# Side matmuls of a four-layer vision stack given all 128 columns and rows of the TensorE array

## The chip, the cores and the metric

The kernel runs on one core of a Trainium2 chip. Five engines work side by side: TensorE multiplies matrices (PE in the profile, its weight loads PEld), VectorE (DVE), ScalarE (ACT) and GpSimd (POOL) work element by element, and SyncE (SP) issues the transfers (DMA). Each engine takes its instructions in the order of the program and stops at one whose inputs are not there. The metric is the device time of the whole kernel in microseconds. Three runs before the change took 17867.69, 17889.07 and 17892.29 us; the median, 17889.07, is the time before.

## What is computed

Eight images of 48 x 48 positions and 96 channels go through four layers, each with a group norm before it and a residual around it. Layers 0 and 3 are two-dimensional state space models, layer 2 is a set of one-dimensional ones along rows and columns, and layer 1 is a small two-layer network on an image that is made wider and lower again by fixed filters. Cut to what matters:

```python
# layers 0 and 3
xz = einsum('bhwc,ec->bhwe', x, in_proj_w); xc, z = split(xz, 2)
xc = silu(depthwise_conv3x3(xc) + conv_b)                       # 192 channels
xs = four directions over the positions
dts, Bs, Cs = split(einsum('bkdl,kcd->bkcl', xs, x_proj), [6, 22])
delta = softplus(einsum('bkrl,kdr->bkdl', dts, dt_projs) + bias)
h = h * exp(delta * A) + (delta * u) * B                        # 16 states a channel
y = sum over the states of h * C, + u * D
y = layer_norm(sum of the four directions) * silu(z)
out = einsum('bhwd,cd->bhwc', y, out_proj_w)
# layer 2: for each of four directions
xi, z = split(x @ in_w); xi = silu(conv1d(xi)); the same scan; y * silu(z) @ outp_w; then @ out_w
# layer 1
h = up(x) @ W1.T; h = c0 + c1 * h + c2 * h * h; out = down(h @ W2.T)
x = x + layer(group_norm(x))                                    # each of the four in turn
```

All numbers are float32.

## The kernel before

The 192 inner channels are held as two halves of 96 (`DH`). The positions of an image are cut into five blocks of 480 or 384 (`BLKS`). With eight images and four directions each scanned layer has 160 blocks.

`scans` (from L192) is the loop that all three scanned layers share. A block is worked in four turns, a turn being six units of 128 partitions by one block (32 channels by 4 states). In a turn ScalarE makes the decay `ps_da` by an exponential (L296), VectorE makes part of the input products `dbu` (L272) and runs the scan in place over two units at a time (L304), GpSimd makes the rest of the input products (also L272) and multiplies the scanned states by C (L310), and TensorE sums over the states in `reduce` (from L318): three matmuls with the 0/1 matrix `w_red`, each on 32 columns of the array (L330), and a fourth with weights of zero on the remaining 32 (L332). The sum `ps_y` of a half block is opened by one matmul (L326), whose operands the layer gives in its `opening`: the skip term in the first direction (`dskip` or `diag`), and in layers 0 and 3 the sum so far through the identity in the other directions. When a half is done, the layer's `done` takes the result away: ScalarE copies it to `ysum` (L716), or in layer 2 VectorE multiplies it by the gate (L876).

Everything else on TensorE is work on the side of that loop, placed by hand at fixed slots of a block (`aside`, `stage1`, `side`): the convolutions (L536, L813, 128 rows by 128 columns already, since their weight rows are padded with zeros and a tap's columns run on into the next tap), the gates (L544, L854), the projection of u to B, C and the step size (`xp`, 96 rows by 38 columns, L675 and L830), the step size's own projection (`dtw`, 6 rows by 96 columns, L665 and L841), the output projections (L885, L607, L610), and the layer norm's mean and spread (L565, L577, L597). In layers 0 and 2 a `Guest` puts layer 1's matmuls into banks that are free in a slot: among them `narrow` (L1117), 128 rows by 73 columns over 96 elements.

TensorE takes all of this in program order. So a sum over states behind a side matmul waits for it, and a side matmul behind a sum waits for GpSimd's product. A float32 matmul stands in the trace as two loads of weights and two matmul records.

The weights lie in tiles of their own (`w_l_in`, `w_l_xp`, `dtw`, `dskip`, `diag`, `wnb`, `wo`) with 96 partitions, or 6. The activations that they meet, `u` and `ysum` (`big`, three buffers), `ub` (three), `bcl` (one), have as many partitions as they have rows.

Of the kernel before, what the change touches and what calls it, by code (L numbers as in the profile page):

```python
# [16 lines left out]
L = H * W  # L17
# [84 lines left out]
def vss_stack_kernel(ctx: ExitStack, tc: tile.TileContext, i: dict, out: bass.AP):  # L102
# [20 lines left out]
    wc = weights(const, ("gmat", "ident", "red"))  # L123
# [4 lines left out]
    mean = const.tile([DH, DH], F32, tag="mean", name="mean")  # L128
    nc.gpsimd.memset(mean, 1.0 / (2 * DH))
# [62 lines left out]
    def scans(dirs, order, restart, on_pool, a, pools, ps, stage1, opening, done, side, tail, ahead=None, guest=None):  # L192
# [125 lines left out]
        def reduce(t, sub):  # L318

            b, q = turns[t]  # L320
            n = b.n
            half, slot = q // 2, 2 * (q % 2) + sub
            if slot == 0:
                ys[b, half] = ps("y", 1)
                lhsT, rhs = opening(b, half)
                nc.tensor.matmul(ys[b, half][:DH, :n], lhsT=lhsT, rhs=rhs, start=True, stop=False)  # L326
            y = ys[b, half]
            hc = units(dbus[t], b, 3 * sub, 3 * sub + 3)
            for g in range(3):
                nc.tensor.matmul(y[32 * g:32 * g + 32, :n], lhsT=wc["red"][:, :32], rhs=hc[:, g, b.at], start=False, stop=(slot == 3))  # L330

            nc.tensor.matmul(y[DH:, :n], lhsT=wc["red"][:, 32:], rhs=hc[:, 2, b.at], start=(slot == 0), stop=(slot == 3))  # L332
            if slot == 3:
                ends.append((b, half))
            if sub == 1:
                dbus.pop(t)
# [101 lines left out]
    def scan_pools(stack):  # L438
        def pool(name, bufs, **kw):
            return stack.enter_context(tc.tile_pool(name=name, bufs=bufs, **kw))  # L440
        ps = pool("ps", 1, space=PSUM)

        def psum(tag, bufs, n=512):
            return ps.tile([P, n], F32, tag=tag, name=f"ps_{tag}", bufs=bufs)

        pools = {"dd": pool("dd", 3), "bc": pool("bc", 1), "dbu": pool("dbu", 4),
                 "dds": pool("dds", 1), "bcl": pool("bcl", 1),
                 "dr": pool("dr", 4, space=DRAM)}
        return pools, psum
# [31 lines left out]
    def ss2d(l, xin, xout, guest=None):  # L481
# [5 lines left out]
        wt, big, zp, lnp, xio = pool("wt", 1), pool("big", 3), pool("z", 1), pool("ln", 2), pool("xio", 1)  # L487
# [8 lines left out]
        w = weights(wt, [f"{l}_{n}" for n in ("in", "cb", "xp", "dtb", "a", "d", "nw", "nb", "out")])  # L496
        dtw = wt.tile([NBC, NK, 2, DH], F32, tag="dtw", name="dtw")
        nc.sync.dma_start(dtw[2 * NS:], i[f"{l}_dtw"])
# [4 lines left out]
        dskip = wt.tile([DH, 2, DH], F32, tag="dskip", name="dskip")  # L503
        for half in range(2):
            nc.scalar.activation(dskip[:, half, :], wc["ident"], AF.Identity, scale=dsum[:, half:half + 1])
# [3 lines left out]
        nc.vector.tensor_mul(taps, taps, w[f"{l}_in"][:, :2 * DH].unsqueeze(1).to_broadcast([DH, 9, 2 * DH]))  # L509

        wnb = wt.tile([DH, 2, C], F32, tag="wnb", name="wnb")
        for half in range(2):
            nc.scalar.activation(wnb[:, half, :], w[f"{l}_out"][:, half, :], AF.Identity, scale=w[f"{l}_nb"][:, half:half + 1])
        us, yss, zs = {}, {}, {}
# [8 lines left out]
        def conv(b, blks, behind=lambda step: step()):  # L523
            if blks[0] == BLKS[0]:
                us[b] = big.tile([DH, 2, L], F32, tag="big", name="u")
                zs[b] = zdr.tile([DH, 2, L], F32, tag="z", name="zd")
            for r0, nr in blks:
                n = nr * SEG
                for half in range(2):
                    for slot in range(7):  # L530
                        if slot == 2:
                            pu = side_psum()
                        for tap in ((), (), (0, 1), (2, 3), (4, 5), (6, 7, 8), ())[slot]:
                            dy, dx = tap // 3, tap % 3
                            at = (2 * tap + half) * DH
                            nc.tensor.matmul(pu[:, :n], lhsT=flat[:, at:at + P],  # L536
                                             rhs=xpad[:, r0 + dy:r0 + dy + nr, dx:dx + W],
                                             start=(tap == 0), stop=(tap == 8))
                        if slot == 6:
                            got = {}  # L540

                            def gate():
                                got["z"] = ps("s1", 1)
                                nc.tensor.matmul(got["z"][:DH, :n], lhsT=w[f"{l}_in"][:, (2 + half) * DH:(3 + half) * DH],  # L544
                                                 rhs=xpad[:C, 1 + r0:1 + r0 + nr, 1:1 + W], start=True, stop=True)
                            behind(gate)
                        yield slot < 2
# [7 lines left out]
        def post(b, blks=BLKS):  # L555
# [4 lines left out]
            for r0, nr in blks:  # L560
# [3 lines left out]
                for half in range(2):  # L564
                    nc.tensor.matmul(pm[:DH, :n], lhsT=mean, rhs=y[:, half, s], start=(half == 0), stop=(half == 1))  # L565
# [20 lines left out]
            for r0, nr in blks:  # L586
# [8 lines left out]
                for c in range(n // CH):  # L595
                    at = r0 * W // CH + c
                    nc.tensor.matmul(pr[:DH, c * CH:(c + 1) * CH], lhsT=var[:, at:at + 1].to_broadcast([CH, DH]),  # L597
                                     rhs=wc["ident"], start=True, stop=True)
# [7 lines left out]
                for half in range(2):  # L606
                    nc.tensor.matmul(po[:C, :n], lhsT=wnb[:, half, :], rhs=z[:, half, :n], start=(half == 0), stop=False)  # L607
                yield
                for half in range(2):
                    nc.tensor.matmul(po[:C, :n], lhsT=w[f"{l}_out"][:, half, :], rhs=y[:, half, s],  # L610
                                     start=False, stop=(half == 1))
# [46 lines left out]
        def stage1(b):  # L658
            n = b.n
            u = b.view(us[b.job], dirs[b.k][0])  # L660
            got = {}

            def raw(half):
                got["p"] = ps("s1", 1)
                nc.tensor.matmul(got["p"][:DH, :n], lhsT=dtw[2 * NS:, b.k, half, :], rhs=b.bcl[2 * NS:, :n],  # L665
# [6 lines left out]
            def s0():  # L672
                got["p"] = ps("s1", 1)
                for half in range(2):
                    nc.tensor.matmul(got["p"][:NBC, :n], lhsT=w[f"{l}_xp"][:, b.k, half, :], rhs=u[:, half],  # L675
                                     start=(half == 0), stop=(half == 1))

            def s1():
                b.bcl = pools["bcl"].tile([NBC, BMAX], F32, tag="bcl", name="bcl")
                nc.scalar.copy(b.bcl[:, :n], got["p"][:NBC, :n])  # L680
# [23 lines left out]
        def so_far(b, half):  # L704
            if b.job not in yss:
                yss[b.job] = big.tile([DH, 2, L], F32, tag="big", name="ysum")
            return b.view(yss[b.job][:, half], dirs[b.k][0])

        def opening(b, half):

            if b.k == 0:
                return dskip[:, half, :], b.view(us[b.job][:, half], False)
            return wc["ident"], so_far(b, half)

        def done(b, half, y):
            nc.scalar.copy(so_far(b, half), rows(y[:DH], b.n))  # L716
# [18 lines left out]
    def lines(xin, xout, guest):  # L735
# [5 lines left out]
        wt, xpool, up, gp = pool("wt", 1), pool("x", 2), pool("u", 3), pool("gated", 1)  # L741
# [26 lines left out]
        w = weights(wt, [f"l2_{n}" for n in ("inz", "cb", "xp", "dtb", "a", "d", "outb")])  # L768
        dtw = wt.tile([NBC, NK, 2, DH], F32, tag="dtw", name="dtw")
        nc.sync.dma_start(dtw[2 * NS:], i["l2_dtw"])  # L770
        a = w["l2_a"]
        negexp(a)
        flat = broadcast(wt, "l2_cw")
        taps = flat[:DH, :NK * 4 * 2 * DH].rearrange("p (k t e) -> p k t e", k=NK, t=4)
        diag = wt.tile([DH, NK, 2, DH], F32, tag="diag", name="diag")
        wo = wt.tile([DH, NK, 2, C], F32, tag="wo", name="wo")
# [20 lines left out]
        def stage1(b):  # L797
# [9 lines left out]
            def conv(half):  # L807
                def run():
                    got["u", half] = ps("sa" if half else "sb", 1)
                    for tap in range(4):  # L810
                        off = tap - 3 if not rev else 3 - tap
                        at = ((b.k * 4 + tap) * 2 + half) * DH
                        nc.tensor.matmul(got["u", half][:, :n], lhsT=flat[:, at:at + P],  # L813
# [3 lines left out]
            def s2():  # L817
                b.ub = up.tile([DH, 2, BMAX], F32, tag="ub", name="ub")
# [8 lines left out]
            def s3():  # L827
                got["p"] = ps("sa", 1)
                for half in range(2):
                    nc.tensor.matmul(got["p"][:NBC, :n], lhsT=w["l2_xp"][:, b.k, half, :], rhs=b.ub[:, half, :n],  # L830
                                     start=(half == 0), stop=(half == 1))

            def s4():
                b.bcl = pools["bcl"].tile([NBC, BMAX], F32, tag="bcl", name="bcl")
                nc.scalar.copy(b.bcl[:, :n], got["p"][:NBC, :n])

            def s5():
                s4()
                for half in range(2):
                    got[half] = ps("sb" if half else "sa", 1)  # L840
                    nc.tensor.matmul(got[half][:DH, :n], lhsT=dtw[2 * NS:, b.k, half, :], rhs=b.bcl[2 * NS:, :n],  # L841
# [9 lines left out]
            def s7():  # L851
                for half in range(2):
                    got["z", half] = ps("sb" if half else "sa", 1)
                    nc.tensor.matmul(got["z", half][:DH, :n], lhsT=w["l2_inz"][:, b.k, half * DH:(half + 1) * DH],  # L854
                                     rhs=shifted(0)[:C], start=True, stop=True)
# [4 lines left out]
            def s8():  # L860
                b.zb = up.tile([DH, 2, BMAX], F32, tag="zb", name="zb", bufs=2)
# [5 lines left out]
        def opening(b, half):  # L867
            return diag[:, b.k, half, :], b.ub[:, half, :b.n]
# [3 lines left out]
        def done(b, half, y):  # L872
# [8 lines left out]
            def project():  # L881
                got["o"] = ps("sa", 1)
                t = gated.pop(b)
                for h in range(2):
                    nc.tensor.matmul(got["o"][:C, :n], lhsT=wo[:, b.k, h, :], rhs=t[:, h, :n], start=(h == 0), stop=(h == 1))  # L885
# [34 lines left out]
    class Guest:  # L920
# [54 lines left out]
        def items(self):  # L975
# [54 lines left out]
            for b in range(nb):  # L1030
# [80 lines left out]
                def narrow(n, j0, j1):  # L1111
                    j1 = min(j1, bands[n][1])

                    def run(p):
                        for j in range(j0, j1):
                            for m in range(NM):
                                nc.tensor.matmul(p[:UG, (j - j0) * C:(j - j0 + 1) * C], lhsT=hq[:, m, j * UG:(j + 1) * UG],  # L1117
# [164 lines left out]
```

## Time and profile before

| what | before |
|---|---|
| median of three runs | 17889.07 us |
| profiled execution, time and span | 17892.97 us, 17891.2 us |
| VectorE: scan L304, products L272 | 11823.5 us x5760, 3828.8 us x2880 |
| GpSimd: L310 | 10071.8 us x3840 |
| ScalarE: exponential L296 | 7424.3 us x11520 |
| TensorE: sums over states L330, L332 | 4741.8 us x23040, 4705.9 us x7680 |
| TensorE: openings L326 | 764.5 us for the sums so far, x960 |
| TensorE: L665, L675 | 952.0 us x1280, 837.5 us x1280 |
| transfers | 2843.63 MB, mean 159 GB/s |

The counts of TensorE's lines are records, two a matmul. The records overlap: four sums over states on different columns run at once, so the busy times of single lines add up to more than the engine's 14657 us. The stretches of time that are named below are counted from the start of the span: layer 0 lasts until about 6075 us, layer 2 until about 12325 us, layer 3 to the end; layer 1 is worked beside layers 0 and 2. A row of a table of stretches ends in four numbers: the granted clock of TensorE as a share of full speed, the share of the transfer engines that is busy, and GB/s; a number with (x...) is busy time with its count of instructions. A wait reads: who waited <- for whom: us in total, times, longest.

### The profile page before, as it was taken

The page shows a single profiled execution, that of the slowest core. Times are in us where ns is not written, and L with a number is a line of the kernel's source. Part 1 is how long each engine was busy: PE and PEld are TensorE (multiplying, and loading weights), DVE is VectorE, ACT ScalarE, POOL GpSimd, SP SyncE. Part 2 cuts the span into 40 slices and gives each one's busy share as a digit, 9 for nine tenths or more (in the row PEclk, how much of TensorE's full clock was granted, in tenths as well). Part 3 has the DMA queues.
Part 4 walks back from the last instruction along what each step waited for, and adds up shares of the span by engine and source line. Part 5 has one row for each costly group of instructions (what it writes and reads, how often), then busy time and mean ns, then how long its engine had stood idle before and what let it go on. Part 6 is the DMA issues. An engine that isn't in the chain of part 4 may idle for free. (4 is left out here: it accounts for less than half of the span.)

```text
span 17891.2 us, 168509 instructions
## 1 busy us (share of the span) xinstructions
PE 14657.1 (82%) x53740; PEld 4413.6 (25%) x53740; DVE 15977.6 (89%) x9976; ACT 13880.5 (78%) x20932; POOL 15155.4 (85%) x7999
## 2 busy tenths in 40 slices
PE   6878888878787788888888888987778778778776
PEld 1223232323232322222222222222122222222221
DVE  7998999898888788787888889996999999999998
ACT  6877878878787677787777778786878778778776
POOL 7988888888888677787777778886999999999998
PEclk7778777878786788888888888888677777777776
DMA  4555545454545334443443444443455455455454
GB/s 141 176 166 171 172 165 170 162 178 159 168 159 174 131 137 153 137 150 133 152 144 140 144 146 156 154 154 124 170 173 173 169 174 176 168 176 177 169 175 142
DMA packets 887917, 2843.63 MB, mean 159 GB/s; under 512 B 353468, under 2 KB 421788, under 8 KB 760206
## 3 DMA queue, kind: packets, MB, share of 16 engines
q1 hardware_dynamic: 887022, 2832.85, 46.7%
q8 instruction: 421, 6.90, 0.2%
q14 instruction: 474, 3.88, 0.1%
HBM read 2384.40 MB, written 448.17 MB: 158 GB/s over the span
## 5 line engine op out<-in xcount | busy, mean ns | idle before, releaser
L304 DVE TENSOR_TENSOR_SCAN dbu<-ps_da,dbu 128x968 f32<-128x968 f32 (+3 forms) x5760 | 11823.5, 2074 | 923.6 <-ACT ps_da L296 757.6
L310 POOL TENSOR_TENSOR dbu<-dbu,bc 128x1440 f32<-128x1440 f32 (+1 forms) x3840 | 10071.8, 2635 | 2349.7 <-DVE dbu L304 2264.9
L296 ACT ACTIVATE ps_da<-dd,w_l_a 128x484 f32<-128x484 f32 (+3 forms) x11520 | 7424.3, 649 | 2511.4 <-DVE dbu L304 2282.1
L330 PE MATMUL ps_y<-dbu,w_red 128*32 128x480 f32 (+1 forms) x23040 | 4741.8, 731 | 1238.5 <-POOL dbu L310 1225.2
L332 PE MATMUL ps_y<-dbu,w_red 128*32 128x480 f32 (+1 forms) x7680 | 4705.9, 731 | 0.0
L272 DVE TENSOR_TENSOR dbu<-dd,ps_b 128x962 f32<-128x962 f32 (+5 forms) x2880 | 3828.8, 1329 | 270.3 <-ACT ps_b L253 160.7
L272 POOL TENSOR_TENSOR dbu<-dd,bc 128x481 f32<-128x481 f32 (+5 forms) x2240 | 3914.8, 1763 | 23.3 <-DMA dd<-dd 18.9
L330 PEld LDWEIGHTS ps_y<-dbu,w_red 128*32 128x32 f32 x23040 | 797.7, 126 | 5072.2 <-POOL dbu L310 2976.6
L253 ACT COPY ps_b<-bc 128x482 f32<-128x482 f32 (+3 forms) x2720 | 1448.3, 532 | 209.9 <-DVE dbu L272 164.4
L536 PE MATMUL ps_side<-xpad,w_l_cw 128*128 128x480 f32 (+1 forms) x2880 | 1466.0, 651 | 42.1 <-ACT g_room L1109 12.7
L296 ACT ACT_TABLE_LOAD x993 | 1274.0, 1283 | 17.4
L665 PE MATMUL ps_s<-bcl,dtw 6*96 6x480 f32 (+1 forms) x1280 | 952.0, 835 | 290.6 <-ACT dds L669 133.5
L813 PE MATMUL ps_sb<-xpad,w_l_cw 128*128 128x480 f32 (+1 forms) x1280 | 879.0, 839 | 90.4 <-ACT g_room L1109 33.7
L326 PE MATMUL ps_y<-ysum,w_ident 96*96 96x480 f32 (+1 forms) x960 | 764.5, 887 | 207.5 <-ACT ysum L716 203.3
L470 POOL TENSOR_TENSOR dds<-dds,u 96x960 f32<-96x960 f32 (+1 forms) x320 | 706.8, 2209 | 209.7 <-ACT dds L693 209.3
L675 PE MATMUL ps_s<-u,w_l_xp 96*38 96x480 f32 (+1 forms) x1280 | 837.5, 785 | 53.1 <-ACT g_room L1109 13.6
L813 PE MATMUL ps_sa<-xpad,w_l_cw 128*128 128x480 f32 (+1 forms) x1280 | 864.6, 826 | 0.1
L536 PEld LDWEIGHTS ps_side<-xpad,w_l_cw 128*128 128x128 f32 x2880 | 579.0, 216 | 890.5 <-issue 784.3
L332 PEld LDWEIGHTS ps_y<-dbu,w_red 128*32 128x32 f32 x7680 | 730.8, 126 | 0.0
L716 ACT COPY ysum<-ps_y 96x480 f32<-96x480 f32 (+1 forms) x640 | 472.0, 738 | 62.9 <-PE ps_y L332 61.5
L830 PE MATMUL ps_sa<-ub,w_l_xp 96*38 96x480 f32 (+1 forms) x640 | 344.3, 669 | 205.1 <-ACT ub L820 205.1
L669 ACT ACTIVATE dds<-ps_s,w_l_dtb 96x480 f32<-96x480 f32 (+1 forms) x640 | 405.5, 634 | 132.8 <-DMA dd<-dds 84.1
(236 smaller groups left out, 12311.2 us busy)
## 6 DMA issues: line engine op xcount, KB each, us to landing
dd<-dd SPq DMA_DIRECT2D x512, 1452.0 KB
bc<-bcd SPq DMA_DIRECT2D x1536, 480.0 KB
dd<-dd SPq DMA_DIRECT2D x256, 1440.0 KB
dd<-dds SPq DMA_DIRECT2D x512, 363.0 KB
dd<-dd SPq DMA_DIRECT2D x128, 1164.0 KB
bc<-bcd SPq DMA_DIRECT2D x384, 384.0 KB
dd<-dds SPq DMA_DIRECT2D x256, 360.0 KB
dd<-dd SPq DMA_DIRECT2D x64, 1152.0 KB
```

The source lines that it names most:

```text
L253: nc.scalar.copy(bps[t][:, :bcs[t][0].shape[1]], bcs[t][0])
L272: engine.tensor_mul(o, du, by.unsqueeze(1).to_broadcast([P, hi - lo, by.shape[1]]))
L296: nc.scalar.activation(da[:, at:at + b.m], b.got[half][:, u % 3, 0, :], AF.Exp, scale=a[:, b.k, ci:ci + 1])
L304: nc.vector.tensor_tensor_scan(db, da, db, 0.0, ALU.mult, ALU.add)
L310: nc.gpsimd.tensor_mul(h, h, bcs.pop(2 * t + sub)[1].unsqueeze(1).to_broadcast([P, 3, n]))
L326: nc.tensor.matmul(ys[b, half][:DH, :n], lhsT=lhsT, rhs=rhs, start=True, stop=False)
L330: nc.tensor.matmul(y[32 * g:32 * g + 32, :n], lhsT=wc["red"][:, :32], rhs=hc[:, g, b.at], start=False, stop=(slot == 3))
L332: nc.tensor.matmul(y[DH:, :n], lhsT=wc["red"][:, 32:], rhs=hc[:, 2, b.at], start=(slot == 0), stop=(slot == 3))
L536: nc.tensor.matmul(pu[:, :n], lhsT=flat[:, at:at + P], rhs=xpad[:, r0 + dy:r0 + dy + nr, dx:dx + W], start=(tap == 0), stop=(tap == 8))
L665: nc.tensor.matmul(got["p"][:DH, :n], lhsT=dtw[2 * NS:, b.k, half, :], rhs=b.bcl[2 * NS:, :n], start=True, stop=True)
L675: nc.tensor.matmul(got["p"][:NBC, :n], lhsT=w[f"{l}_xp"][:, b.k, half, :], rhs=u[:, half], start=(half == 0), stop=(half == 1))
L813: nc.tensor.matmul(got["u", half][:, :n], lhsT=flat[:, at:at + P], rhs=shifted(off), start=(tap == 0), stop=(tap == 3))
```

## The change

Each side matmul is given 128 weight columns, and 128 rows where the buffer of its moving operand has them. The weights of a layer move into one tile of 128 partitions, `square`, which is cleared and then filled; `wide(name, n)` hands out 128 columns from it, so that those past the matrix are the next matrix's or zeros, and their outputs are never read. The moving operands get 128 partitions, of which the upper 32 (for `bcl` all but 38) are zeros that are set once.

```diff
+    eye = const.tile([P, P], F32, tag="eye", name="eye")
+    nc.gpsimd.memset(eye, 0.0)
+    nc.sync.dma_start(eye[:C, :C], i["ident"])
...
+    def square(pool, sizes):
+        t = pool.tile([P, sum(sizes.values()) + P - DH], F32, tag="square", name="square")
+        nc.gpsimd.memset(t, 0.0)
+        at = dict(zip(sizes, np.cumsum([0, *sizes.values()]).tolist()))
+        def wide(name, n, rows_=P):
+            return t[:rows_, at[name] + n:at[name] + n + P]
+        def part(name, rows_=slice(0, DH)):
+            return t[rows_, at[name]:at[name] + sizes[name]]
+        return wide, part
+    def full(pool, tag, n, bufs):
+        made = []
+        for b in range(bufs):
+            t = pool.tile([P, n], F32, tag=f"{tag}{b}", name=f"{tag}{b}")
+            nc.gpsimd.memset(t[DH:], 0.0)
+            made.append(t)
+        return made
...
-                nc.tensor.matmul(ys[b, half][:DH, :n], lhsT=lhsT, rhs=rhs, start=True, stop=False)
+                nc.tensor.matmul(ys[b, half][:, :n], lhsT=lhsT, rhs=rhs, start=True, stop=False)
...
-            nc.tensor.matmul(y[DH:, :n], lhsT=wc["red"][:, 32:], rhs=hc[:, 2, b.at], start=(slot == 0), stop=(slot == 3))
+            nc.tensor.matmul(y[DH:, :n], lhsT=wc["red"][:, 32:], rhs=hc[:, 2, b.at], start=False, stop=(slot == 3))
...
+        pools["bcl"] = pool("bcl", 1).tile([P, BMAX], F32, tag="bcl", name="bcl")
+        nc.gpsimd.memset(pools["bcl"], 0.0)
...
+        wide, part = square(wt, {"in": 4 * DH, "xp": 2 * NK * NBC, "dtw": 2 * NK * DH, "out": 2 * C, "wnb": 2 * C, "dskip": 2 * DH})
+        bigs = full(pool("big", 1), "big", 2 * L, 3)
...
-                                nc.tensor.matmul(got["z"][:DH, :n], lhsT=w[f"{l}_in"][:, (2 + half) * DH:(3 + half) * DH],
-                                                 rhs=xpad[:C, 1 + r0:1 + r0 + nr, 1:1 + W], start=True, stop=True)
+                                nc.tensor.matmul(got["z"][:, :n], lhsT=wide("in", (2 + half) * DH),
+                                                 rhs=xpad[:, 1 + r0:1 + r0 + nr, 1:1 + W], start=True, stop=True)
...
-                nc.tensor.matmul(got["p"][:DH, :n], lhsT=dtw[2 * NS:, b.k, half, :], rhs=b.bcl[2 * NS:, :n],
+                nc.tensor.matmul(got["p"][:, :n], lhsT=wide("dtw", (2 * b.k + half) * DH), rhs=b.bcl[:, :n],
                                  start=True, stop=True)
...
-                    nc.tensor.matmul(got["p"][:NBC, :n], lhsT=w[f"{l}_xp"][:, b.k, half, :], rhs=u[:, half],
+                    nc.tensor.matmul(got["p"][:, :n], lhsT=wide("xp", (2 * b.k + half) * NBC), rhs=uall[:, half],
                                      start=(half == 0), stop=(half == 1))
...
-            return wc["ident"], so_far(b, half)
+            return eye, so_far(b, half)
...
+                            cols = min(P, UR * UG - j * UG)
                             for m in range(NM):
-                                nc.tensor.matmul(p[:UG, (j - j0) * C:(j - j0 + 1) * C], lhsT=hq[:, m, j * UG:(j + 1) * UG],
+                                nc.tensor.matmul(p[:cols, (j - j0) * C:(j - j0 + 1) * C], lhsT=hq[:, m, j * UG:j * UG + cols],
                                                  rhs=w2q[:, m, :], start=(m == 0), stop=(m == NM - 1))
```

Layer 2 is treated in the same way: `wide` stands for `w_l_inz`, `w_l_xp`, `dtw`, `diag` and `wo` (L854, L830, L841, L326, L885), with a tile `square` of 6480 columns, and its three `ub` buffers get 128 partitions. The output projection of the gate's constant part (L607) and that of layer 2 (L885) get 128 columns over 96 rows, since their moving operands keep 96 partitions; so does L597. The mean (L565) gets a 128 x 128 matrix, of which rows 0 to 95 hold 1/192. Not touched are the convolutions, the sums over states, the norm's small matmuls (L159, L577) and the guest's other matmuls.

## The prediction

> **What bounds the kernel now.** I read the page's busy shares and its clock row first, then the windows of the three stages, the waits of VectorE, the TensorE timeline of single stretches, and the granted clock window by window.
>
> ```profile
> span 17891.2 us, 168509 instructions
> PE 14657.1 (82%) x53740; PEld 4413.6 (25%) x53740; DVE 15977.6 (89%) x9976; ACT 13880.5 (78%) x20932; POOL 15155.4 (85%) x7999
> ...
> PEclk7778777878786788888888888888677777777776
> ```
>
> VectorE is the busiest and TensorE is granted only 0.777 of its clock on average. The stages (microseconds of the stretch, then busy time of PE, PEld, DVE, ACT, POOL, then the granted clock):
>
> ```profile
> 0.00:6075.00 6075.00, 4940.60 (x20066) 1675.09 (x20066) 5335.77 (x3311) 4705.11 (x7317) 5143.79 (x2898) 0.77 0.50 164
> 6075.00:12325.00 6250.00, 5396.06 (x18251) 1600.57 (x18250) 5413.92 (x3468) 4849.79 (x7082) 4907.29 (x2234) 0.83 0.41 146
> 12325.00:17891.00 5566.00, 4320.44 (x15424) 1137.93 (x15424) 5227.94 (x3199) 4325.55 (x6534) 5104.28 (x2869) 0.72 0.49 168
> ```
>
> VectorE idles 739 us in layer 0 (with layer 1 as guest), 836 us in layer 2 (guest too), 338 us in layer 3. TensorE's speed can win back only a part of these 1913 us. In layer 2 the waits of VectorE name it:
>
> ```profile
> DVE dbu L304 <- ACT ps_da L296: 327.4, 335, 2.8
> DVE gated L876 <- PE ps_y L332: 238.0, 127, 5.8
> DVE x L893 <- PE ps_sa L885: 181.3, 76, 4.5
> ...
> DVE x L891 <- PE ps_sa L885: 33.5, 31, 3.1
> ```
>
> The reader sees three places where VectorE stands for a matmul, and one for ScalarE. Following each wait for ScalarE back to the last gap in ScalarE's own queue, 185 us of layer 2's and 166 us of layer 0's end at a gap in which ScalarE itself waited for a matmul. Direct and through ScalarE, VectorE's idle time owed to TensorE is then 281 us in layer 0 (115 + 166), 638 in layer 2 (453 + 185), 88 in layer 3 (82 + 6): 1007 us.
>
> **Why TensorE is late.** The granted clock takes two values, 0.50 and 1.00, and changes on a grid of 3.41 us. A 128x128 convolution record of 480 elements follows the one before it after 403 ns at 1.00 and after 800 ns at 0.50. Of the 1007 us, 844 fall into windows at 0.50 or into the first two windows after a rise (259, 510 and 75 us by stage); 195 of the 215 us of L893 and L891 fall into the very first. So VectorE pays for what TensorE fell behind in slow windows.
>
> **What sets the clock.** Here a rule of the Trainium skill stands against a row. "TensorE: Matmul & The Clock Gate", section "The HAM clock gate", says that a monitor releases the clock after about one window of 3.4 us in which the PE was busy. By that rule zero rows and unread columns change nothing: a matmul streams as long with 96 columns as with 128, busy time stays, the clock stays 0.777, and the change costs only longer weight loads. The trace differs. Three windows of layer 3:
>
> ```profile
> 13292.94:13296.35 3.41, 3.41 (x5) 1.35 (x6) 3.41 (x3) 1.82 (x3) 3.41 (x3) 0.50 0.74 261
> 13296.35:13299.76 3.41, 3.41 (x6) 0.93 (x5) 3.41 (x3) 2.11 (x4) 3.02 (x3) 0.50 0.65 258
> 13299.76:13303.18 3.42, 3.42 (x14) 0.72 (x17) 3.42 (x4) 2.21 (x4) 3.42 (x2) 0.50 0.60 194
> ```
>
> What ran in them:
>
> ```profile
> 13292.85 3.52 PE L607 MATMUL ps_side<-zin,wnb 96*96 96x480 f32 x4
> 13296.16 3.41 PE L610 MATMUL ps_side<-ysum,w_l_out 96*96 96x480 f32 x4
> ```
>
> TensorE is busy throughout and the clock stays at 0.50. At the start of layer 3, one window full of 128*128 convolution is enough:
>
> ```profile
> 12350.86:12354.27 3.41, 3.39 (x5) 1.55 (x6) 0.00 (x0) 3.39 (x5) 0.00 (x0) 0.50 0.02 5
> 12354.27:12357.68 3.41, 3.41 (x10) 1.67 (x9) 0.00 (x0) 0.44 (x1) 0.00 (x0) 1.00 0.00 0
> ```
>
> So I summed for every window of the trace rows x columns / 128 squared (each rounded up to 32) over the streaming time, and asked what the next window's clock was. At 0.50: below a sum of 0.50 it rose after 1% of windows, at 0.60 to 0.70 after 39%, at 0.70 to 0.80 after 82%, above 0.80 after 99.7%. At 1.00 it stayed after 1% of windows below 0.20, 67% at 0.30 to 0.40, 97% at 0.40 to 0.50. One threshold each (0.69 to rise, 0.33 to fall) calls 91% and 93% of the windows right; plain busy time calls 84% and 87%. The convolution is itself evidence for padding: its rows 96 to 127 are zeros in both operands, and counted as 96 rows the rule calls fewer windows right (89% and 91%). I take the trace.
>
> **The change part by part.**
> 1. *Wider operands.* The same streaming time, a larger sum: 96*96 counts 0.56 and becomes 1.00 (opening L326, gates L544 and L854, L565, L610); 6*96 counts 0.19 and becomes 1.00 (L665, L841); 96*38 counts 0.38 and becomes 1.00 (L675, L830); L607, L885, L597 become 0.75. Giving every matmul of the trace its new sum and running the two thresholds over the windows (an estimate; on the old sums it returns 0.767 where 0.777 was granted) gives 0.86 in layer 0, 0.93 in layer 2, 0.83 in layer 3, **0.88** overall. Slow windows fall from 46% to 28%, from 33% to 13%, from 56% to 33%: 39%, 61% and 40% of them go.
> 2. *What that is worth.* In proportion, 259 x 0.39 + 510 x 0.61 + 75 x 0.40 = 101 + 311 + 30 = 442 us of VectorE's idle time. Below it: the slow windows that stay may be those that hurt (0). Above it: the windows that go are the ones full of side work, where VectorE waits, so up to the whole 844. I keep 442 as what goes.
> 3. *What is late next.* With TensorE in time, VectorE in layer 2 still has L304 behind ScalarE; ScalarE waits 740 us for scan rooms there, POOL 1311 us for scans, so neither is full, and VectorE's 5414 busy us in 6250 leave room. A scan that comes earlier meets the next release earlier only if ScalarE's tables and POOL's 2.7 us products keep up; in layer 3, where they nearly must, VectorE is at 94% of the stage. I take a quarter back: 442 x 0.75 = 330 us.
> 4. *Longer weight loads.* At full clock a load's record lasts 114 ns for 38 columns, 163 for 96, 189 for 128. The loads are hidden behind the streaming before them except at a burst's head: L665's second record follows after 480 ns where 400 stream, the convolution's after 507. So the exposed part is 80 ns for 96 columns and 107 for 128: +27 ns, +75 for 38 columns, twice a burst: 2720 bursts x 54 + 480 x 150 ns = 219 us of TensorE's time, spread over the span beside 2 us products. That is cover as long as TensorE idles before its products (L330 waits 1225 us for POOL); without cover it lengthens a wait by 0.05 to 0.15 us.
> 5. *The guest's narrow L1117.* 3504 records of 96 elements, 83 ns apart, with 73 columns; they become 128. No row has 128 columns with so short a stream. Nearest is L1162: 96 columns over 48 elements, 85 ns apart, so the load sets the pace (80 + 5). The skill's page, section "LDWEIGHTS (loading the stationary operand)", makes a load columns / 1.2 ns, hence 107 ns for 128; with the same 5, 112 ns. Bounds 0 and 29 ns a record; I take 29: 102 us of TensorE. ScalarE waits for L1117 some 200 us in all, each time for 18 records, so 0.5 us later where it waits. This eats part of the quarter in point 3. L597 likewise, 768 x 27 ns = 21 us.
> 6. *Start of a stage.* POOL clears the weight tile (2064 columns, near the 2500 of the padded image at 2.18 us: 1.8 us; 6480 in layer 2: 5.6, of which 2.7 replace an old clearing) and three buffers of 4608 columns (12 us a layer, beside the convolutions of the start, when POOL has nothing to do). Weight loads on SP stand behind the clearing: 2 to 5 us a stage, some 8 us. L332 in slot 0 no longer opens its own columns; the opening now writes them: nothing.
> 7. *Waits.* The compiled order on the five engines is unchanged but for the clearings. TensorE waits for its own earlier matmul in some 250 more places, on a bank whose result ScalarE has already read: nothing.
>
> Sum: 17893.0 (the profiled execution; its span is 17891.2) - 330 + 8 = 17571; the median of the runs shown is 4 us lower: **17565 us**, 1.8% less.
>
> **Rivals.**
> - *The clock rises, VectorE barely gains.* For it: in layer 3 VectorE is busy 94% of the stage, and inside each stage its busy share is no lower in slow windows (0.88 at 0.50, 0.86 at 1.00 in layer 2). Against: the waits pile up right after a rise. A quarter of 442: 17,780.
> - *Backlog goes entirely.* All 844 less a quarter, 630: 17,260. For it: wide side work lifts its own window. Against: a rise still needs one slow window first.
> - *The padding does not count.* Zero weights switch nothing; the clock stays near 0.78, and loads hide: 17,890. Against: the convolution's zero rows.
> - *Slower: weight loads at TensorE's head of line.* As before, but the 342 us of points 4 and 5 come in the 1 in 4 bursts whose result is waited for, half as much again at half clock: +130 us, 18,020. It decides if the clock stays under about 0.79 and L1117's spacing goes to 112 ns or more. Against: the clock count above.
>
> **Numbers.** Forecast 0.58, small gain 0.20, whole backlog 0.10, no effect 0.06, slower 0.06. A difference under 0.2% can't be told from none here. Small gain lies mostly above 0.2%: faster 0.86, same 0.08, slower 0.06. Range: from near the whole-backlog case to the small gain, 17,290 to 17,835.
>
> **What would show it.** Right: granted clock 0.86 to 0.90, highest in layer 2; VectorE's waits at L876, L893 and L891 (453 us) under half; layer 2 shortened most, layer 3 least. Step 1 is wrong if the clock stays under 0.80; steps 2 and 3 are wrong if it rises and VectorE's idle time stays at 1900 us; step 5 is wrong if L1117 stays at 83 ns.

## The result and the profile after

The changed kernel takes 17734.6 us (median of 4 runs, 17729.41 to 17754.35) against 17890.68 us (17867.69 to 17893.46): a ratio of 0.9918, 95% interval 0.99 to 0.9935. It is 156 us faster, where 322 were forecast (330 won back, 8 lost at the starts of stages). The page after, in the lines that were shown of before:

```profile
span 17727.6 us, 168890 instructions
PE 13790.2 (78%) x53740; PEld 4743.1 (27%) x53740; DVE 15966.8 (90%) x9976; ACT 13871.7 (78%) x20932; POOL 15188.7 (86%) x8015
...
PEclk7878888989797888988889898998878878778877
```

TensorE's busy time fell by 867 us with the same number of matmuls, its loads grew by 330 us, and the mean granted clock rose from 0.777 to 0.848. The other engines do what they did. The stages, cut where a stage clears its padded image (5996 and 12324 us before, 5887 and 12164 after); the columns are those of the stage rows above. Before, then after:

```profile
0.00:5996.00 5996.00, 4901.35 (x19986) 1659.12 (x19986) 5310.90 (x3284) 4667.84 (x7254) 5113.86 (x2876) 0.77 0.50 165
5996.00:12324.00 6328.00, 5435.09 (x18330) 1616.54 (x18330) 5438.07 (x3494) 4887.06 (x7144) 4936.65 (x2254) 0.83 0.41 145
12324.00:17891.00 5567.00, 4320.68 (x15425) 1137.93 (x15424) 5228.67 (x3199) 4325.55 (x6534) 5104.85 (x2869) 0.72 0.49 168
```

```profile
0.00:5887.00 5887.00, 4609.06 (x19986) 1777.42 (x19986) 5302.88 (x3284) 4662.12 (x7254) 5126.98 (x2885) 0.85 0.51 168
5887.00:12164.00 6277.00, 5124.46 (x18330) 1732.91 (x18330) 5436.42 (x3494) 4886.04 (x7144) 4943.14 (x2258) 0.89 0.41 146
12164.00:17727.00 5563.00, 4056.68 (x15424) 1232.73 (x15424) 5227.48 (x3199) 4323.57 (x6534) 5118.57 (x2873) 0.80 0.49 169
```

So layer 0 gave 109 us, layer 2 only 51 and layer 3 next to nothing (3 us). In layer 0 the gain came for the most part through ScalarE (before, then after), while VectorE's direct waits for TensorE fell only from 114 to 100 us:

```profile
DVE dbu L304 <- ACT ps_da L296: 343.1, 273, 4.8
```

```profile
DVE dbu L331 <- ACT ps_da L323: 265.6, 249, 4.5
```

Layer 2 was to give most. Its waits of VectorE after the change:

```profile
DVE dbu L331 <- ACT ps_da L323: 359.9, 323, 3.3
DVE gated L919 <- PE ps_y L359: 221.7, 91, 6.3
DVE x L936 <- PE ps_sa L928: 124.4, 85, 3.5
...
DVE x L934 <- PE ps_sa L928: 32.3, 30, 2.4
```

L919, L936 and L934 are before's L876, L893 and L891. The three waits together fell from 451 to 378 us, the one for ScalarE rose from 332 to 360 (before, at these cuts). One of them in the timeline (start, duration, engine, line), in a stretch whose granted clock is 1.00 throughout; the first line is a burst of the same eight records in another direction:

```profile
7533.53 3.49 PE L854 MATMUL ps_sb<-xpad,square 128*128 128x480 f32 x8 [0.66 <-ACT g_room L1152]
...
7912.23 7.74 PE L854 MATMUL ps_sb<-xpad,square 128*128 128x480 f32 x8 [0.64 <-ACT g_room L1169]
...
7919.79 0.80 PE L1150 MATMUL ps_sa<-g_room,g_w 96*128 96x365 f32 x2
...
7920.52 0.60 PE L357 MATMUL ps_y<-dbu,w_red 128*32 128x480 f32 x3
...
7920.63 0.57 ACT L1152 ACTIVATE g_room<-ps_sa,g_b 128x365 f32<-128x365 f32 x1 [5.82 <-PE ps_sa L1150]
...
7922.40 0.65 DVE L919 TENSOR_TENSOR gated<-zb,ps_y 96x480 f32<-96x480 f32 x1 [3.84 <-PE ps_y L359]
```

Eight records of convolution take 7.74 us at full clock, where the other eight take 3.49 us. The sums over states stand behind them in TensorE's queue, ScalarE is idle 5.82 us for the guest's matmul and VectorE 3.84 us for the sums. The last slow window had ended at 7906.64 us, 5.6 us before this convolution began, and TensorE had nothing left over from it: it stood still for 0.64 us just before.

This made a new theory, **S**: in layer 2's third and fourth directions, which read the padded image by columns (each next element lies a whole padded row, 51 elements, further on), a convolution record takes some 940 ns at either clock, and what VectorE waits for stands in the queue behind it. Its rivals: **C**, the slow windows that are left are the ones that cost; **N**, the guest's longer loads gave the gain back.

### The profile page after: what moved, and what is told of

The parts are those of the page before. It is cut to its first block, busy times and chain, and to the rows that moved or that the text cites. A ratio compares the mean times of both kernels' runs of the same rounds, so it can differ in the third digit from the quotient of the medians.

```text
span 17727.6 us, 168890 instructions
## 1 busy us (share of the span) xinstructions
PE 13790.2 (78%) x53740; PEld 4743.1 (27%) x53740; DVE 15966.8 (90%) x9976; ACT 13871.7 (78%) x20932; POOL 15188.7 (86%) x8015
## 4 chain that ended last, share of the span: by engine, by line
PE 22%; ACT 19%; POOL 19%; DVE 18%; issue 13%; DMA 8%; SPq 1%; POOLq 0%; ACTq 0%; DVEq 0%
POOL dbu L337 12%; DVE dbu L331 12%; ACT ps_da L323 7%; DVE dbu L299 5%; POOL dbu L299 4%; PE ps_y L357 4%; PE ps_sb L854 3%; PE ps_sa L854 3%; DMA dd<-dds 3%; ACT L323 3%; POOL dds L499 2%; DMA dd<-dd 2%; ACT ps_b L280 1%; PE ps_sa L873 1%; PE ps_sa L928 1%
## 5 line engine op out<-in xcount | busy, mean ns | idle before, releaser
L357 PE MATMUL ps_y<-dbu,w_red 128*32 128x480 f32 (+1 forms) x23040 | 4215.5, 654 | 1532.5 <-POOL dbu L337 1503.5
L359 PE MATMUL ps_y<-dbu,w_red 128*32 128x480 f32 (+1 forms) x7680 | 4178.0, 653 | 0.0
L357 PEld LDWEIGHTS ps_y<-dbu,w_red 128*32 128x32 f32 x23040 | 731.1, 118 | 5001.5 <-POOL dbu L337 3241.6
L574 PE MATMUL ps_side<-xpad,w_l_cw 128*128 128x480 f32 (+1 forms) x2880 | 1337.6, 603 | 49.6 <-ACT g_room L1152 18.1
L703 PE MATMUL ps_s<-bcl,square 128*128 128x480 f32 (+1 forms) x1280 | 885.1, 782 | 326.0 <-ACT dds L707 170.3
L854 PE MATMUL ps_sb<-xpad,square 128*128 128x480 f32 (+1 forms) x1280 | 892.9, 851 | 86.5 <-ACT g_room L1152 30.9
L353 PE MATMUL ps_y<-big,eye 128*128 128x480 f32 (+1 forms) x960 | 748.5, 868 | 237.1 <-ACT big L754 232.6
L713 PE MATMUL ps_s<-big,square 128*128 128x480 f32 (+1 forms) x1280 | 847.6, 793 | 65.6 <-ACT g_room L1152 18.5
L854 PE MATMUL ps_sa<-xpad,square 128*128 128x480 f32 (+1 forms) x1280 | 865.3, 827 | 0.0
L499 POOL TENSOR_TENSOR dds<-dds,big 96x960 f32<-96x960 f32 (+1 forms) x320 | 706.5, 2208 | 165.5 <-ACT dds L731 165.2
L359 PEld LDWEIGHTS ps_y<-dbu,w_red 128*32 128x32 f32 x7680 | 667.8, 118 | 0.0
L897 PE MATMUL ps_sa<-xpad,square 128*128 128x480 f32 (+1 forms) x320 | 279.8, 965 | 295.4 <-ACT g_room L1152 99.6
L873 PE MATMUL ps_sa<-ub,square 128*128 128x480 f32 (+1 forms) x640 | 355.0, 686 | 194.8 <-ACT ub L863 194.8
```

Source lines behind the costliest of these rows:

```text
L499: nc.gpsimd.tensor_mul(du, dt, u)
L574: nc.tensor.matmul(pu[:, :n], lhsT=flat[:, at:at + P], rhs=xpad[:, r0 + dy:r0 + dy + nr, dx:dx + W], start=(tap == 0), stop=(tap == 8))
L703: nc.tensor.matmul(got["p"][:, :n], lhsT=wide("dtw", (2 * b.k + half) * DH), rhs=b.bcl[:, :n], start=True, stop=True)
L713: nc.tensor.matmul(got["p"][:, :n], lhsT=wide("xp", (2 * b.k + half) * NBC), rhs=uall[:, half], start=(half == 0), stop=(half == 1))
L854: nc.tensor.matmul(got["u", half][:, :n], lhsT=wide("cw", at), rhs=shifted(off), start=(tap == 0), stop=(tap == 3))
```

## Experiments

The runs' "before" beside them lay at 17883 to 17896 us. The lengths of layers are those of the profiled execution, from one clearing to the next; the rows of stretches are cut at whole microseconds. Layer 0 is the same code in the kernels narrow73, split and columns and took 5866 to 5871 us there; in the changed kernel and after_rows, again the same code, it took 5887 and 5905. So a stage is known to about 20 us, and a difference of that size in one stage proves little by itself.

**1. Undo the guest's part (narrow73).**

```diff
-                            cols = min(P, UR * UG - j * UG)
+                            cols = UG
```

> The changed kernel with the guest's narrow matmul (L1161) back at 73 columns; all else stays. Theory N (the longer weight loads of this line gave the gain in layer 2 back: 3504 records went from 83 to 112 ns): layer 2 is 60 to 120 us shorter than the changed kernel's 6277, the whole near 17,630. Theory S (VectorE waits in layer 2 for sums that stand in TensorE's queue behind convolutions whose pace does not follow the clock) and theory C (the slow windows that stay are the ones that cost): 10 to 40 us, the whole at 17,695 to 17,725. In all, spacing 83 ns again, clock 0.84 to 0.85.

17685.4 us, ratio 0.9888 (0.9874 to 0.9901): 49 us faster than the changed kernel, layer 2 at 6246 us, layer 0 at 5871. The clock stays at 0.847. The largest group of the line, in the changed kernel and then in this one (line, engine, tiles, rows*columns, elements, count, then busy us, mean ns and idle time before it):

```profile
L1161 PE MATMUL ps_side<-g_w2q,g_room 128*128 128x96 f32 x1122 | 165.6, 305 | 32.7 <-ACT g_room L1145 9.4 <-ACT g_room L1163 6.1 <-ACT big L587 5.5
```

```profile
L1161 PE MATMUL ps_side<-g_w2q,g_room 128*73 128x96 f32 x1380 | 155.5, 274 | 38.5 <-ACT g_room L1145 12.3 <-ACT g_room L1163 7.6 <-ACT big L587 5.7
```

Widened records started 112 ns apart at full clock (213 at half), narrow ones 83. The whole lies between N's forecast and that of S and C, the 32 us in layer 2 within that of S and C: N is a part of the miss, not the whole of it.

**2. The guest's part alone (before_narrow128).** The kernel before, with the lines of the diff's last hunk.

> The kernel before with the guest's narrow matmul alone at 128 columns. The longer loads: 2832 of 3504 records at 112 instead of 83 ns at full clock and 213 instead of 160 at half, some 90 to 110 us of TensorE; undoing it won 49 us in the changed kernel. Theory: slower by 30 to 80 us, 17,920 to 17,970, clock within 0.01 of 0.777. If the wider columns lift the clock enough to pay for the loads: within 20 us.

17951.9 us, ratio 1.0032 (1.0021 to 1.0044): 56 us slower, at an unchanged clock of 0.777. The same part costs 49 to 56 us from both sides, though not in the same stage: here layer 0 is 46 us longer and layer 2 only 4. It brought no clock. In the prediction's sum, 96 elements stream for some 80 ns (480 take 400): 73 columns count as 96, 0.75 x 80/83 = 0.72 of a window, and 128 columns 1.00 x 80/112 = 0.71. Wide as it is, the record fills no more (an estimate from the spacings measured).

**3. Keep the clock up with zeros (fill).**

```diff
+            if sub == 0:
+                nc.tensor.matmul(y[:, :n], lhsT=zeros.to_broadcast([P, P]), rhs=hc[:, 0, b.at], start=False, stop=False)
```

> The changed kernel with one more matmul of zero weights, 128 x 128 over the block, added into the sum over states in the first half of each turn (0.8 us of TensorE a turn at full clock), only to keep the clock up. Theory C: clock at 0.97 or more, VectorE's waits at L919, L936 and L934 in layer 2 (378 us in the changed kernel) under 200 us, the whole at 17,450 to 17,620. Theory S: clock as high, those waits still over 300 us, the whole at 17,680 to 17,850, since the zeros stand in the same queue.

18027.8 us, ratio 1.0078 (1.0065 to 1.009). The clock rose to 0.912, short of the 0.97 that both theories had written down, and the kernel is 293 us slower than the changed one, outside both forecasts. Layer 2 and its waits:

```profile
5994.00:12457.00 6463.00, 5629.50 (x19610) 1791.98 (x19610) 5448.27 (x3493) 4884.15 (x7144) 4940.72 (x2258) 0.94 0.40 142
```

```profile
DVE dbu L334 <- ACT ps_da L326: 407.2, 333, 3.3
DVE gated L924 <- PE ps_y L362: 310.0, 121, 7.2
DVE x L941 <- PE ps_sa L933: 160.7, 72, 4.6
```

With the clock at 0.94 instead of 0.89, the same three waits are 509 us (310.0 + 160.7 + 38.2 for L939) instead of 378. The zeros lengthen the queue, so this does not tell what a free rise of the clock would be worth, and it does not decide between C and S; it does show that 505 us more of TensorE's busy time in layer 2 outweigh the rise by 186 us of layer 2.

**4. Take the strided reading away (before_rows, after_rows).** In layer 2, third and fourth direction, convolutions and gates read along rows; so these directions compute something else and the kernels serve as tests only.

```diff
-                v = shift(xp, off, 0).rearrange("p h w -> p w h") if col else shift(xp, 0, off)
+                v = shift(xp, 0, off)
```

> The kernel before with the same reading along rows in layer 2 (its third and fourth direction again not the reference's). Theory S: layer 2 goes from 6328 to about 6150 us without any help from the clock; and the difference between this kernel and the changed one with the same reading is larger than the 51 us of layer 2 now, 70 to 120, since the clock then sets the pace of all convolutions. Theory C: layer 2 within 40 us of 6328.

> The changed kernel with layer 2's convolutions and gates reading the padded image along rows in all four directions, so that its third and fourth direction compute something else than the reference. Theory S: no convolution record takes 940 ns any more, layer 2 goes from 6277 to about 6100 us and the waits at L919, L936 and L934 from 378 to about 260, as in the first two directions now. Theory C: reading does not matter, layer 2 within 40 us of 6277.

Before with it: 17573.7 us, ratio 0.9823 (0.981 to 0.9837), layer 2 at 6021 us from 6328. The changed kernel with it: 17468.6 us, 0.9767 (0.9752 to 0.9782), layer 2 at 5999 from 6277. Layer 2 of the first:

```profile
5982.00:12003.00 6021.00, 4868.48 (x18330) 1615.82 (x18330) 5435.50 (x3495) 4878.02 (x7144) 4932.07 (x2255) 0.80 0.43 153
```

```profile
DVE dbu L304 <- ACT ps_da L296: 216.9, 275, 3.3
DVE x L893 <- PE ps_sa L885: 111.5, 73, 4.0
...
DVE gated L876 <- PE ps_y L332: 81.6, 90, 5.4
DVE x L891 <- PE ps_sa L885: 40.0, 33, 3.2
```

Layer 2 of the second:

```profile
5905.00:11904.00 5999.00, 4560.50 (x18330) 1732.77 (x18330) 5431.55 (x3494) 4877.24 (x7144) 4938.96 (x2259) 0.87 0.43 153
```

```profile
DVE dbu L331 <- ACT ps_da L323: 253.3, 248, 3.3
DVE x L936 <- PE ps_sa L928: 113.0, 98, 2.8
...
DVE gated L919 <- PE ps_y L359: 41.1, 28, 5.4
DVE x L934 <- PE ps_sa L928: 30.2, 34, 2.1
```

In the first, the clock is lower than before (0.80 from 0.83), and yet the three waits halve, 451 to 233 us, the one for ScalarE falls by 115, and layer 2 is 307 us shorter, where C wanted it within 40 us. TensorE's busy time in layer 2 fell by 567 us; how much of that is the convolutions and how much the gates, which read in the same way, was not tried apart. S forecast this length too timidly, and its second half failed: with every convolution paced by the clock, the change should be worth more in layer 2, 70 to 120 us, and was worth 23, which is the size of a stage's own spread. From the first kernel to the second the wait for the gate halves again (82 to 41 us), while the one for ScalarE goes from 217 to 253.

**5. The same with the guest's part undone (rows_narrow73).**

> The changed kernel with layer 2's convolutions and gates reading along rows (third and fourth direction not the reference's) and the guest's narrow matmul at 73 columns. It gives the padding's own worth in layer 2 when no convolution is held at 940 ns and no load is longer in the guest: against 6021 us of the kernel before with the same reading. If slow windows were a large part of the wait (theory C), layer 2 falls by 120 us or more, to 5900 or less. If the queue's order is what VectorE waits for (theory S), by 30 to 70 us, to 5950 to 5990, and the whole lands near 17,420.

17428.4 us, ratio 0.9743 (0.9729 to 0.9758), layer 2 at 5986 us:

```profile
5869.00:11856.00 5987.00, 4565.72 (x18330) 1714.35 (x18330) 5424.24 (x3494) 4876.71 (x7144) 4940.96 (x2259) 0.86 0.43 154
```

The padding is worth 35 us of layer 2 here, at the low end of S and far from the 120 us or more of C. So slow windows were no large part of what layer 2 waits for once its reads are in order.

**6. Half the convolution at a time (split).** On narrow73; `conv` is given the taps that it does.

```diff
-            return {3: conv(0), 4: conv(1), 6: s2s3, 7: s5, 8: s6, 9: s7, 10: s8}
+            def middle():
+                conv(0, (2, 3))()
+                conv(1, (0, 1))()
+            return {3: conv(0, (0, 1)), 4: middle, 5: conv(1, (2, 3)), 6: s2s3, 7: s5, 8: s6, 9: s7, 10: s8}
```

> The kernel narrow73 (changed, guest's narrow at 73 columns) with each half's four convolution taps of layer 2 laid over two slots instead of one: the same matmuls and the same clock, but half as much convolution at a time ahead of a sum over states. Theory S: the wait at L919 falls from 209 to about 110 us, layer 2 by 60 to 130 us, the whole to 17,560 to 17,625 from 17,685. Theory C: same work, same clock, within 25 us of 17,685.

17707.9 us, ratio 0.9899 (0.9883 to 0.9916), 22 us slower than narrow73, where S wanted 60 to 125 less and C wanted it within 25: C's number came true. Layer 2, the waits of VectorE and of ScalarE in narrow73 and then here:

```profile
DVE dbu L331 <- ACT ps_da L323: 345.8, 321, 3.3
DVE gated L919 <- PE ps_y L359: 209.4, 91, 5.8
...
ACT ub L863 <- PE ps_sa L854: 59.9, 62, 2.6
```


```profile
DVE dbu L331 <- ACT ps_da L323: 531.8, 337, 6.6
DVE x L941 <- PE ps_sa L933: 121.7, 85, 3.2
...
DVE gated L924 <- PE ps_y L359: 44.5, 31, 5.4
...
ACT ub L864 <- PE ps_sa L855: 233.5, 72, 5.5
```

The wait for the gate did what S said, 209 to 45 us. But the wait for ScalarE took its place, 346 to 532: slots 4 and 5 have no sum between them in TensorE's queue, so twelve records stand together there, and ScalarE now waits 233 us for the convolution's end (60 before). So the number was C's, but not for C's reason, that nothing changes: one wait was exchanged for another. This speaks for the amount of TensorE's time in the queue rather than for one place in it.

**7. The result of the reference, read in order (columns, columns_split, before_columns).** Layer 2 has two padded images, which served alternate images. Now one is kept by rows, the other by columns; ScalarE copies one into the other, and the next image's norm comes in the second half of the present one. The reading changes as in experiment 4; the lines that move the norm are left out here.

```diff
-            xp = xpads[b.job % 2]
+            xp = xpads[1 if col else 0]
...
+            for r0, nr in BLKS:
+                nc.scalar.copy(shift(xpads[1], 0, 0)[:C, r0:r0 + nr, :],
+                               shift(xpads[0], 0, 0)[:C].rearrange("p h w -> p w h")[:, r0:r0 + nr, :])
```

> The kernel narrow73 with the right numbers and no strided convolution: of the two padded images of layer 2 one is kept by rows, the other by columns (five copies on ScalarE an image, some 5 to 8 us, and the next image's norm is made in the second half of the present one). Theory S: layer 2 at 5990 to 6060 us, 30 to 70 above the kernel that reads along rows throughout, the whole at 17,440 to 17,510. If the copies land on the path of the decays, up to 60 us more.

> The kernel columns with the taps laid over two slots. Theory S: with the convolutions at 402 ns a record at full clock most of the wait at L919 is gone already, so 0 to 40 us less than columns. Theory C: within 25 us of columns.

> The kernel before, no padding, with layer 2's second padded image kept by columns as in the run columns. If TensorE's time ahead of what VectorE waits for is what counts, not the share of slow windows, most of the gain comes without the padding, at a clock no higher than before's 0.83 in layer 2: layer 2 at 6030 to 6090 us, the whole at 17,580 to 17,630, and the padding is worth 30 to 60 us of layer 2 and 110 to 130 of layer 0. If slow windows count, layer 2 stays over 6150 us.

On the changed kernel with the guest's part undone: 17459.4 us, ratio 0.9763 (0.9748 to 0.9777); with the taps split 17453.0, 0.9758 (0.9743 to 0.9772), no different. On the kernel before, without padding: 17607.1 us, 0.9841 (0.9828 to 0.9855). Convolution records in columns, then layer 2 in before_columns and in columns:

```profile
9306.19 3.49 PE L854 MATMUL ps_sb<-xpad,square 128*128 128x480 f32 x8 [0.48 <-ACT g_room L1176]
```

```profile
5984.00:12028.00 6044.00, 4865.59 (x18331) 1611.94 (x18330) 5442.83 (x3495) 4917.28 (x7184) 4932.36 (x2255) 0.80 0.43 152
```

```profile
5866.00:11892.00 6026.00, 4542.01 (x18330) 1710.93 (x18330) 5438.72 (x3494) 4916.14 (x7184) 4940.78 (x2259) 0.87 0.43 153
```

So most of the gain in layer 2 comes without the padding, at a clock of 0.80. The padding brings 140 to 148 us in all (by the ratios and by the medians), 118 of them in layer 0, as forecast, and 18 in layer 2, where 30 to 60 were forecast: no more than a stage's own spread. The kernel columns is 424 us faster than the kernel before and 275 us faster than the changed one.

## Why the prediction was right and wrong

**The clock: right in kind, a little high.** The array's filled share was the better rule, busy time the weaker one. On the trace after, one threshold on rows x columns calls 95% of the slow and 97% of the full windows right (at 0.73 and 0.36, from 0.69 and 0.33 before); TensorE's busy time, with its own best thresholds, calls 88% and 94%. Forecast were 0.86, 0.93 and 0.83 by stage and 0.88 in all, measured 0.85, 0.89, 0.80 and 0.848. A part of what is missing is L1117, which I counted as filled by its columns; experiment 2 shows no rise from it. More lies in the thresholds: run over the sums of the trace after, those of the prediction return 0.870, those that fit this trace 0.850.

**The size: wrong, in part 2.** "In proportion, 259 x 0.39 + 510 x 0.61 + 75 x 0.40 = 101 + 311 + 30 = 442 us", of which 330 were kept: by stage 76, 233 and 22. Measured were 109, 51 and 3, and with the guest's part undone 124, 83 and 1. The term that failed is layer 2's 311, and both of its factors were off.

The first is the share of slow windows that go: 39%, 61% and 40% were taken, and 31%, 37% and 29% went. With these shares the same sum is 80 + 189 + 22 = 291 us, three quarters of it 218. That this is near the 208 us measured with the guest's part undone is luck: by stage it gives 60, 141 and 16, where 124, 83 and 1 came. Layer 0 gave twice its part, layer 2 little more than half.

The second is the 510 us themselves. Waits in slow windows and in the first two after a rise were taken for waits owed to the slow clock. Counted by the window in which they end, layer 2's direct waits of this kind fell from 348 to 305 us, 12%, though slow windows fell by 37%; those after a rise fell from 302 to 269. In experiment 4, with reads in order and no padding, slow windows are 39% of layer 2 instead of 34%, and yet these waits are only 223 us, those after a rise 136. So a large part of them hung on how long the reads by columns hold TensorE, and layer 2 became 307 us shorter at a lower clock. That side work which fills TensorE makes both the rise of the clock and the wait, so that they stand side by side without one causing the other, is how I read this; no run sets it apart.

**What is late next: named, not sized.** A quarter was to come back. In layer 0 nothing did, by the sum with the measured shares (80 us, and 109 came). In layer 2 with reads in order, the padding lowered the direct waits by 49 us (233 to 184), and the wait of L304 for ScalarE rose by 36. Following all of VectorE's waits for ScalarE there (229 and 272 us) back to ScalarE's last gap, the part that begins at a matmul is 125 us in both kernels; what grew leads to VectorE's own work (97 to 121) and to transfers (7 to 27). So the padding's small worth in layer 2 is not explained by the reads by columns, which are gone here: what VectorE gained at the matmuls it gave back mostly in its exchange with ScalarE. Why it is so much more there than in layer 0 stays open.

**Longer loads: right by the nanosecond, wrong in price.** 112 ns were estimated for L1117 and 112 measured; 672 records at the end of a band keep 73 columns, so 2832 are longer and not 3504. They were put into the quarter of point 3, as if TensorE had cover; experiments 1 and 2 price them at 49 to 56 us of the end. The other loads' price was not tried alone.

**Start of a stage and waits: not seen to cost.** Layer 3 is as long as before, the clearings included.

**The signs.** The clock, at 0.848, lies just under the 0.86 to 0.90 named; the three waits of layer 2 are 378 us and not under half of 453; layer 0 was shortened most, not layer 2; and VectorE's idle time fell from 1913 to 1761 us, less than half of what was to go. The last step of the sum has a slip that changes nothing: 4 us under 17571 is 17567, not 17565.

**The rivals.** "The clock rises, VectorE barely gains" gave 17,780, nearer than the forecast, and is what layer 3 and layer 2 did; layer 0 did more than the forecast. "The padding does not count" is refuted by the rise of the clock itself, and by fill for weights of zero. "Slower" had a cost that is real, in the wrong balance: L1117's loads took about a quarter of the padding's some 200 us.

## What to carry to other kernels

A wait that ends just after the clock rises is no proof that the slow clock made it, so look first at how long the matmul ahead of it takes at full clock. If that time is the same at both clocks, lay out the moving operand so that it is read in order before thinking about the clock. Padding to the full array paid here in layer 0 (118 to 124 us), where streams are mostly of 480 elements; where it made the weight load longer than the stream, as in L1117 (96 elements, records 83 and then 112 ns apart), it cost time and brought no clock.

## What was not expected of the hardware

Zeros count as work for the clock. In fill the clock rose from 0.848 to 0.912, and counting the matmul of zero weights as 128 x 128 calls 94% and 98% of the windows right with one threshold each, counting it as nothing 69% and 93%.

The pace of a matmul can come from how its operand lies. Convolution records by columns of the padded image, 480 elements whose neighbours lie 51 elements apart, mostly started 940 ns apart at full clock and 937 at half; in order (before_rows) they start 403 and 800 apart. L675 and L326, which read by columns of the image with neighbours 48 elements apart, mostly start 803 and 789 ns apart at full clock. How these two read was not changed in any run, so what it costs is not shown.
